# An S5 block and an adaptive-norm attention layer: another way through the last layer norm, and the last four heads in one group

## The chip, the cores and the metric

The kernel runs on one core of a Trainium2 chip. The metric is the device time of one execution in microseconds (us), lower is better. TensorE (PE in the profile, with PEld for its weight loads), VectorE (DVE), ScalarE (ACT) and GpSimd (POOL) each work through their own queue in order; SyncE (SP) issues the DMAs. Results of TensorE land in PSUM[...].

## The reference

The input is x of shape (2, 2048, 512) and a condition vector for each of the two batches. A first layer (a state-space block and a feed-forward with GELU) makes `hidden`. The second layer is what the change touches, and of it only what follows the attention:

```python
att = softmax(q @ k.T) / D ** 0.5            # 16 heads of width 32
out = (att @ v) joined over heads
out = out @ Wp.T + bp
h1  = out + hidden
h2  = gamma * ((h1 - mean) / sqrt(var + EPS) * ln_g + ln_b) + beta
return h2 + h1
```

Mean and variance are those of a row of 512 features; gamma and beta come from the condition vector. Written with one row g = gamma * ln_g and one row t = gamma * ln_b + beta for each batch, the output is (h1 - mean) * rstd * g + h1 + t.

## The kernel before

**Phases.** The first layer runs up to about 1480 us. Then attention runs over 64 blocks, each one batch, one pair of heads and one chunk of 512 queries: 32 blocks of the first batch, 32 of the last. At the end of the last batch the blocks are reordered, so that its chunks 0, 1 and 2 are complete before chunk 3.

**Slots.** A block takes 8 slots (`NP`). Slot j = 8 n + i is slot i of block n. In a slot, in program order: what is due at j, `make` (PE scores `s`, VectorE subtracts the maximum out of PSUM into `pT`; not in slots 0 and 4), `across` (PE `m`, VectorE reduces it, L785), `exponentials` on ScalarE, `keep` for the block 15 slots ahead (PE scores, ScalarE copies them to SBUF, L766, VectorE takes the running maximum, L771; twice in slots 0 and 4, and with no maximum in slot 1), another `exponentials`, what is due at j + 0.5 (`closing`), `take_off` on GpSimd (L814, the kept scores of the next slot), and `weighted` (PE `o`, L835, for the slot before). Every engine's queue is in this order. `after(j, f)` puts a step at the head of slot j, `closing(j, f)` near its end.

**Maxima.** `turn_run` turns the running maximum by four PE transposes per head into a PSUM bank and VectorE reduces it (L792), for head 0 of block n at slot 8n - 6 (slot 2), for head 1 at 8n - 4 (slot 4). `spread` at 8n - 3 (slot 5) turns the negated maximum again (L802) and sends it through DRAM to all partitions as `shift`, which `take_off` needs.

**PSUM.** The tag "pt" is one bank with one buffer. `turn_run`, `spread`, the projection `py` of the first batch and `z` share it: each waits until the one before has been read. "m" is one buffer too, for `across` and for the last batch's `py`; "s" has two.

**Last norm of a tile (128 rows).** `fetch` loads the outputs of all heads (`o4`), the inverted sums (`by`, four DMAs) and `hidden` (`xr`). `divide` multiplies on GpSimd. `project` makes four products with `wp`. `residual` adds on VectorE into SBUF. `statistics` takes mean and variance and the start of an inverse square root. `newton` makes one turn in three 128x1 ScalarE activations, in all nine and one for the shift; `last_norm` writes z = (h - mean) * rstd on ScalarE into a "pt" bank; `gain` multiplies z by g and adds h on VectorE; `close` adds t on GpSimd and issues the output DMA.

**Where they are due.** The 16 tiles of the first batch are closed during the last batch's blocks: two tiles in three blocks, 24 blocks in all. The last batch's own tiles 0 to 11 follow each other every two slots in its last blocks (k, k + 2, ...): the products of one at slot k + 3, ScalarE's Newton at the ends of k + 3 and k + 4, z at the end of k + 4, the gain at k + 5 or its end, close at the end of k + 6.

**The end.** The last chunk's four tiles are projected apart (`end_*`): heads 12 and 13 are divided by GpSimd and projected as a group of their own (`end_project(i, [NG - 1])`), heads 14 and 15 come straight from the last block's PSUM output, are inverted on VectorE (L1037) and multiplied with a weight tile that has zeros elsewhere (L1047). Then come statistics, `rsqrt` on VectorE, z on ScalarE in place, gain and addition.

Of the kernel before, what the change touches and what calls it, by code (L numbers as in the profile page):

```python
# [39 lines left out]
def tile_s5_block_then_sln_attention(  # L40
# [48 lines left out]
    four = const.tile([P, NB], F32, name="four")  # L89
    one_half = const.tile([P, 1], F32, name="one_half")  # L90
    nc.gpsimd.memset(one_half, 1.5)

# [783 lines left out]
    def fetch(b, qt):  # L876

        at = slice(qt * P, (qt + 1) * P)
        o4 = work.tile([P, NG, P], F32, name="o4")
        nc.sync.dma_start(o4, od[b][:, at].rearrange("(g r) q -> r g q", r=P))  # L880
        by = work.tile([P, NG, P], F32, name="by")
        heads = invd[b][:, at].rearrange("(g j) q -> j g q", j=4)
        for j in range(4):
            nc.sync.dma_start(
                by[32 * j : 32 * j + 32, :, :], heads[j : j + 1, :, :].to_broadcast([32, NG, P])
            )
        xr = work.tile([P, D], F32, name="xr", bufs=4)
        nc.sync.dma_start(xr, x2[b][at, :])
        held[b, qt] = o4, by, xr
# [19 lines left out]
    def residual(b, qt):  # L909

        o4, h, py = held[b, qt]
        nc.vector.tensor_add(h, py, h)
        held[b, qt] = h

    def statistics(b, qt):

        h = held[b, qt]
        st = small.tile([P, 6], F32, name="st3")
        nc.vector.bn_stats(st, h)
        mv = small.tile([P, 2], F32, name="mv3")  # L920
        nc.vector.bn_aggr(mv, st)
        v = small.tile([P, 1], F32, name="v3")
        y = small.tile([P, 1], F32, name="scale3", bufs=4)
        shift = small.tile([P, 1], F32, name="shift3", bufs=4)
        nc.vector.tensor_scalar(v, mv[:, 1:2], EPS, None, ALU.add)
        nc.vector.tensor_scalar(
            y.bitcast(I32), v.bitcast(I32), -0.5, float(0x5F3759DF), ALU.mult, ALU.add
        )
        nc.vector.tensor_scalar(v, v, -0.5, None, ALU.mult)
        nc.vector.tensor_scalar(shift, mv[:, 0:1], -1.0, None, ALU.mult)  # L930
        held[b, qt] = h, y, shift, v

    def newton(b, qt, turns, final):

        h, y, shift, v = held[b, qt]
        for _ in range(turns):
            c = small.tile([P, 1], F32, name="c3")
            nc.scalar.activation(c, y, AF.Identity, scale=y)
            nc.scalar.activation(c, c, AF.Identity, bias=one_half, scale=v)
            nc.scalar.activation(y, c, AF.Identity, scale=y)  # L940
        if final:
            nc.scalar.activation(shift, shift, AF.Identity, scale=y)

    def last_norm(b, qt):

        h, scale, shift, _ = held[b, qt]
        z = ps.tile([P, CH], F32, name="z", tag="pt")
        nc.scalar.activation(z, h, AF.Identity, bias=shift, scale=scale)
        held[b, qt] = h, z

    def gain(b, qt):

        h, z = held[b, qt]
        nc.vector.tensor_tensor(z, z, ending[b][0], ALU.mult)
        nc.vector.tensor_tensor(h, z, h, ALU.add)

    def close(b, qt):

        h, z = held.pop((b, qt))
        nc.gpsimd.tensor_tensor(h, h, ending[b][1], ALU.add)  # L960
        nc.sync.dma_start(out[b, qt * P : (qt + 1) * P, :], h)

# [8 lines left out]
    def end_fetch():  # L971
# [9 lines left out]
        for t in range(TT):  # L981
            at = slice((LC * TT + t) * P, (LC * TT + t + 1) * P)
            nc.sync.dma_start(ends["h"][t // 2][:, t % 2, :], x2[LB][at, :])
        late = P - 2 * HD
        nc.gpsimd.memset(ends["o"][1][late:, 1, :], 0.0)
        nc.gpsimd.memset(ends["w"], 0.0)
        nc.gpsimd.tensor_copy(ends["turn"], ident)
        for e in range(2):
            to, of = 3 * HD * e, HD + HD * e
            nc.sync.dma_start(ends["w"][to : to + HD, :], wp[late + HD * e : late + HD * e + HD, NG - 1, :])  # L990
            nc.gpsimd.tensor_copy(ends["turn"][:, to : to + HD], ident[:, of : of + HD])

    def end_fetch_more():
        cols = slice(LC * CH, (LC + 1) * CH)
        nc.sync.dma_start(ends["o"][1][: P // 2, 1, :], od[LB][D - P : D - P // 2, cols])

    def end_divisors(heads):
        cols = slice(LC * CH, (LC + 1) * CH)
        for j in heads:
            at = slice(HD * (j % 4), HD * (j % 4) + HD)  # L1000
            nc.sync.dma_start(
                ends["by"][j // 8][at, j // 4 % 2, :], invd[LB][j : j + 1, cols].to_broadcast([HD, CH])
            )

    def end_divide(g, rows=P):
        o, by = ends["o"][g // 2][:rows, g % 2, :], ends["by"][g // 2][:rows, g % 2, :]
        nc.gpsimd.tensor_tensor(o, o, by, ALU.mult)
# [19 lines left out]
    def end_last(o):  # L1027
        raw, inv, on = (spare(n)[:, 0, :] for n in ("raw4", "inv4", "on4"))
        turned = ps.tile([P, 2, 2 * P], F32, name="turned", tag="pt")
# [6 lines left out]
        for i, at in enumerate(parts):  # L1036
            nc.vector.reciprocal(inv[:, at], turned[:, i, :])  # L1037
            nc.vector.tensor_tensor(on[:, at], o[:, at], inv[:, at], ALU.mult)
        end_project(1, list(range(NG - 1)))
        for i in range(2):  # L1040
            end_project(i, [NG - 1])
        mv = small.tile([P, TT, 2], F32, name="mv4")
        hts = [spare("ht01"), spare("ht23")]
        g_row, t_row = ending[LB]
        for i in range(2):
# [4 lines left out]
            for t in (2 * i, 2 * i + 1):  # L1050
                st = small.tile([P, 6], F32, name="st3")
                nc.vector.bn_stats(st, ends["py", i][:, t % 2, :])
                nc.vector.bn_aggr(mv[:, t, :], st)
            nc.scalar.copy(hts[i], ends["py", i])
        v = small.tile([P, TT], F32, name="v4")
        scale = small.tile([P, TT], F32, name="scale4")
        shift = small.tile([P, TT], F32, name="shift4")
        nc.vector.tensor_scalar(v, mv[:, :, 1], EPS, None, ALU.add)
        rsqrt(v, scale, TT)
        nc.vector.scalar_tensor_tensor(shift, mv[:, :, 0], -1.0, scale, ALU.mult, ALU.mult)  # L1060
        for t in range(TT):
            z = ends["py", t // 2][:, t % 2, :]
            nc.scalar.activation(
                z, z, AF.Identity, bias=shift[:, t : t + 1], scale=scale[:, t : t + 1]
            )
        for t in range(TT):
            qt = LC * TT + t
            y, z = hts[t // 2][:, t % 2, :], ends["py", t // 2][:, t % 2, :]
            nc.vector.tensor_tensor(z, z, g_row, ALU.mult)
            nc.vector.tensor_tensor(y, z, y, ALU.add)  # L1070
            (nc.gpsimd if t < TT - 1 else nc.vector).tensor_tensor(y, y, t_row, ALU.add)
            nc.sync.dma_start(out[LB, qt * P : (qt + 1) * P, :], y)

# [34 lines left out]
    FIRST = -AHEAD - 8  # L1108
    SPREAD = -3
    OPEN = -4  # L1110
# [4 lines left out]
    for n in range(N):  # L1115
        after(max(FIRST + 1 + n, NP * n - AHEAD - 6), load_q, n)
        after(NP * n - AHEAD + NP + 1, turn_run, n, 0)
        after(NP * n - AHEAD + NP + 3, turn_run, n, 1)
        after(NP * n + SPREAD, spread, n)
    for b in range(NB):  # L1120
        for c in range(NQ):
            j = NP * (blocks.index((b, NPAIR - 1, c)) + 1) + 1
            if (b, c) == (LB, LC):
# [7 lines left out]
                after(j + 4, invert, b, c, rest, 32)  # L1131
                after(j + 5, end_divisors, range(NH - 4, NH - 2))
                for g in range(NG - 1):
                    after(j + 3 + g, end_divide, g)
                after(j + 8, end_divide, NG - 1, P // 2)
                after(j + 6, end_begin, 0)
# [7 lines left out]
            for t in range(TT):  # L1144
                qt = c * TT + t
                if b == LB:
# [5 lines left out]
                    after(k + 3, statistics, b, qt)  # L1152
                    closing(k + 3, newton, b, qt, 2, False)
                    closing(k + 4, newton, b, qt, 1, True)
                    closing(k + 4, last_norm, b, qt)

                    (after if (k + 5 - SPREAD) % NP == 0 else closing)(k + 5, gain, b, qt)
                    closing(k + 6, close, b, qt)
                else:

                    k = NP * (NPAIR * NQ * (b + 1) + 2 + 3 * qt // 2) + 3
                    after(k - 2, fetch, b, qt)
                    after(k + 2, divide, b, qt)
                    for g in range(NG):
                        after(k + 3 + g, project, b, qt, (g,))
                    closing(k + 6, residual, b, qt)
                    closing(k + 7, statistics, b, qt)
                    for i in range(3):
                        closing(k + 8 + i, newton, b, qt, 1, i == 2)

                    k += 2 if t % 2 else 8
                    closing(k + 10, last_norm, b, qt)
                    closing(k + 11, gain, b, qt)
                    after(k + 13, close, b, qt)

# [119 lines left out]
```

## Time and profile before

| what | us |
| --- | --- |
| median of three runs | 3533.81 (3532.12 to 3534.32) |
| the profiled execution, its own time | 3533.44 |
| its span, from the first to the last instruction | 3531.7 |
| PE, VectorE, ScalarE, GpSimd busy in the span | 3378.7, 2204.6, 1976.7, 1943.5 |
| PE's share of the chain that ended last | 71% |

The span is what the trace covers; the profiled execution's own time is 1.7 us longer. A busy share is an average over very different stages. In the attention PE and VectorE are both nearly full; what one stage costs is read from stretches of it. A line of the timeline gives start, duration, engine, line of the kernel, operation, output and inputs, shape and, in brackets, how long the engine idled before it and what ended that. A line of the waits gives who waited for whom, us in total, how often, and the longest.

### The profile page before, as it was taken

How to read it: one execution, taken by the hardware profiler on the slowest of the kernel's cores; microseconds unless marked ns; L12 is line 12 of the kernel's file. 1: busy time of each engine (PE TensorE's matmuls, PEld its weight loads, DVE VectorE, ACT ScalarE, POOL GpSimd, SP SyncE). 2: the span in 40 equal slices, each digit the busy share in tenths (PEclk: the TensorE clock that was granted, in tenths of full speed). 3: DMA queues.
4: the chain of work that ended last, by engine and by line, in shares of the span. 5: the costliest groups of instructions: out<-in, count | busy, mean ns of one | idle time of the engine just before them, and what ended most of it. 6: DMA issues, size and time to landing. Idle time of an engine off the chain costs nothing.

```text
span 3531.7 us, 34142 instructions
## 1 busy us (share of the span) xinstructions
PE 3378.7 (96%) x11772; PEld 1534.2 (43%) x11772; DVE 2204.6 (62%) x2937; ACT 1976.7 (56%) x2430; POOL 1943.5 (55%) x982
## 2 busy tenths in 40 slices
PE   7999999999999999899999999999999999999977
PEld 4444444444444444444444444444444444444432
DVE  6233232323232212689999999998888888888864
ACT  2111111111111111488888888888888888888865
POOL 4223131313131311288877888888687787777764
PEclk8999999999999999999999999999999999999999
DMA  8001111111111012332213222222233333323222
GB/s 298 1 30 42 48 39 45 39 50 37 48 36 42 33 45 74 99 71 65 71 50 73 71 65 65 53 72 66 68 85 84 81 76 79 88 71 80 61 89 93
DMA packets 201542, 236.92 MB, mean 67 GB/s; under 512 B 89755, under 2 KB 118939, under 8 KB 197273
## 3 DMA queue, kind: packets, MB, share of 16 engines
q1 hardware_dynamic: 201368, 234.74, 23.9%
q8 instruction: 93, 1.52, 0.2%
q14 instruction: 81, 0.66, 0.1%
HBM read 166.77 MB, written 67.76 MB: 66 GB/s over the span
## 4 chain that ended last, share of the span: by engine, by line
PE 71%; DVE 14%; ACT 11%; issue 2%; DMA 1%; POOL 1%; SPq 0%; DVEq 0%; ACTq 0%; POOLq 0%
PE o L835 14%; PE ph L489 13%; PE po L502 12%; PE s L755 9%; DVE run L771 8%; PE pk L532 6%; ACT x L766 4%; PE pv L544 3%; PE py L906 3%; ACT x L825 3%; PE m L780 2%; ACT pT L825 2%; DVE pT L820 2%; PE pt_run L791 2%; PE pu L423 2%
## 5 line engine op out<-in xcount | busy, mean ns | idle before, releaser
L814 POOL TENSOR_TENSOR x<-x,shift 128x1024 f32<-128x1024 f32 x640 | 1502.7, 2388 | 343.4 <-DMA shift<-flat 269.4
L766 ACT COPY x<-s 128x1024 f32<-128x1024 f32 x640 | 633.7, 1011 | 234.0 <-PE s L755 232.3
L755 PE MATMUL s<-qs,ks 128*128 128x512 f32 x2048 | 703.1, 433 | 51.7 <-DVE run L771 46.8
L825 ACT ACTIVATE x<-x 128x1024 f32<-128x1024 f32 x640 | 675.9, 1057 | 6.7 <-POOL x L814 6.6
L771 DVE TENSOR_TENSOR run<-s,run 128x1024 f32<-128x1024 f32 x512 | 625.4, 1221 | 82.1 <-ACT x L766 64.4
L835 PE MATMUL o<-x,v 128*64 128x512 f32 x2560 | 664.2, 614 | 2.0 <-ACT raw L844 2.0
L820 DVE TENSOR_TENSOR pT<-s,shift 128x1024 f32<-128x1024 f32 x384 | 467.6, 1218 | 55.0 <-PE s L755 50.4
L785 DVE TENSOR_REDUCE top<-m 128x1 f32<-128x768 f32 x512 | 485.8, 949 | 25.7 <-PE m L780 25.4
L755 PEld LDWEIGHTS s<-qs,ks 128*128 128x128 f32 x2048 | 344.9, 189 | 312.2 <-DVE run L771 143.3
L489 PE MATMUL ph<-fT,w_sb 128*128 128x512 f32 x1024 | 462.5, 596 | 0.0
L502 PE MATMUL po<-w_sb,hid 128*128 128x512 f32 x1024 | 460.3, 592 | 0.0
L825 ACT ACTIVATE pT<-pT 128x1024 f32<-128x1024 f32 x384 | 407.0, 1060 | 50.2 <-DVE pT L820 50.2
L493 ACT ACTIVATE hid<-ph,vec 128x512 f32<-128x512 f32 x128 | 87.9, 687 | 595.1 <-PE ph L489 595.1
L835 PE MATMUL o<-pT,v 128*64 128x512 f32 x1536 | 395.2, 593 | 3.8 <-ACT pT L825 3.8
L160 DVE SCALAR_TENSOR_TENSOR lo<-pk,vec,hi 128x512 fp32r<-128x512 f32 x64 | 48.1, 751 | 503.3 <-ACT hi L159 497.4
L780 PE MATMUL m<-ks,qs 128*128 128x384 f32 x1024 | 285.8, 360 | 16.3 <-DVE top L785 14.4
L489 PEld LDWEIGHTS ph<-fT,w_sb 128*128 128x128 f32 x1024 | 193.0, 192 | 228.2 <-issue 228.2
L502 PEld LDWEIGHTS po<-w_sb,hid 128*128 128x128 f32 x1024 | 190.7, 190 | 221.5 <-issue 221.5
L159 ACT ACTIVATE hi<-pk,vec 128x512 fp32r<-128x512 f32 x64 | 44.0, 687 | 393.3 <-PE pk L532 388.8
L436 POOL TENSOR_TENSOR m<-m,m 128x512 f32<-128x512 f32 x8 | 13.1, 1643 | 448.9 <-DVE m L434 448.9
L835 PEld LDWEIGHTS o<-x,v 128*64 128x64 f32 x2560 | 138.5, 135 | 260.7 <-issue 146.3
L512 POOL TENSOR_TENSOR x<-x,gated 128x512 f32<-128x512 f32 x32 | 39.6, 1268 | 354.3 <-DVE gated L511 354.3
(252 smaller groups left out, 2857.9 us busy)
## 6 DMA issues: line engine op xcount, KB each, us to landing
ks<-kd SPq DMA_DIRECT2D x128, 256.0 KB
qs<-qd SPq DMA_DIRECT2D x512, 64.0 KB
shift<-flat SPq DMA_DIRECT2D x64, 512.0 KB
x<-in_x SPq DMA_DIRECT2D x8, 1024.0 KB
w_sb<-in_w SPq DMA_DIRECT2D x8, 1024.0 KB
x<-x SPq DMA_DIRECT2D x8, 1024.0 KB
kd<-hi SPq DMA_DIRECT2D x32, 256.0 KB
kd<-lo SPq DMA_DIRECT2D x32, 256.0 KB
```

What stands on the lines that cost most here:

```text
L489: nc.tensor.matmul(ph, w1_sb[:, k, f * P : (f + 1) * P], fts[b, c][:, k, :], start=k == 0, stop=k == KC - 1)
L502: nc.tensor.matmul(pos[b, c][:, t, :], hid[:, t * P : (t + 1) * P], w2_sb[:, f, :], start=f == 0, stop=f == FC - 1,)
L532: nc.tensor.matmul(pk, w[:, k, g * P : (g + 1) * P], hT[:, k, :], start=k == 0, stop=k == KC - 1)
L755: nc.tensor.matmul(s[:, e, :], kst[pair_of[n], e][:, kt * P : (kt + 1) * P], qst[n][:, e, :], start=True, stop=True,)
L766: nc.scalar.copy(x, s)
L771: nc.vector.tensor_tensor(runs[n], s, kept[n, 0] if kt == 1 else runs[n], ALU.max)
L780: nc.tensor.matmul(m[:, i, :YW], qst[n][:, e, t * P : (t + 1) * P], kst[pair_of[n], e][:, k : k + YW], start=True, stop=True,)
L785: nc.vector.tensor_reduce(tops[n][:, j, 0:1], m[:, :, :YW], AX.XY, ALU.max, negate=True)
L814: nc.gpsimd.tensor_tensor(x, x, shifts[n], ALU.add)
L820: nc.vector.tensor_tensor(x, s, shifts[n], ALU.add)
L825: nc.scalar.activation(x, x, AF.Exp)
L835: nc.tensor.matmul(outs[n][64 * e : 64 * e + 64, :], v[:, kt, e : e + 2, :], x[:, e, :], start=first, stop=final,)
```

## The change

For the first batch, h stays in the PSUM tile of its projection. VectorE makes w = (h - mean) * g (into the buffer of `o4`) and ht = h + t (into that of `xr`); GpSimd makes the three Newton turns in six 128x1 operations; ScalarE scales w by rstd once; GpSimd adds w and ht. z and its bank are gone. The tile's steps are moved: first product in slot 5 (at its end), the second and third at the ends of slots 6 and 7, the fourth at the head of slot 0, residual and statistics at the end of slot 0, `gain` at the end of slot 1, GpSimd's turns in slot 3, `scaled` at the end of slot 4, `close` in slot 6.

For the last batch's tiles 0 to 11, Newton is on VectorE (`deviation`, seven 128x1 operations at slot k + 4), z on ScalarE and the multiply by g on VectorE are issued together at k + 5, into a new SBUF tile y, and GpSimd makes both additions at k + 6.

In all blocks the first `turn_run` is one slot later (slot 3). At the end, the last four heads form one group of 128 rows: the divided heads 12 and 13 stand in the middle 64 rows, the inverted heads 14 and 15 in the outer ones, so that the separate group's products go. The last norm has the same form as the first batch's, with Newton on GpSimd in 13 128x4 operations.

```diff
@@ tiles
-        xr = work.tile([P, D], F32, name="xr", bufs=4)
+        xr = work.tile([P, D], F32, name="xr", bufs=3)
@@ residual
-        nc.vector.tensor_add(h, py, h)
+        if b == LB:
+            nc.vector.tensor_add(xr, py, xr)
+            held[b, qt] = xr, xr, None
+        else:
+            nc.vector.tensor_add(py, py, xr)
+            held[b, qt] = py, xr, o4.rearrange("p g q -> p (g q)")
@@ newton and what follows
-            nc.scalar.activation(c, y, AF.Identity, scale=y)
-            nc.scalar.activation(c, c, AF.Identity, bias=one_half, scale=v)
-            nc.scalar.activation(y, c, AF.Identity, scale=y)
+    def newton(eng, y, v):
+        for _ in range(3):
+            c = small.tile([P, 1], F32, name="c3")
+            eng.tensor_scalar(c, y, y, v, ALU.mult, ALU.mult)
+            eng.tensor_scalar(y, c, 1.5, y, ALU.add, ALU.mult)
+    def turns(b, qt):
+        newton(nc.gpsimd, *held[b, qt][-2:])
+    def gain(b, qt):
+        h, ht, w, mv, y, v = held[b, qt]
+        nc.vector.scalar_tensor_tensor(w, h, mv[:, 0:1], ending[b][0], ALU.subtract, ALU.mult)
+        nc.vector.tensor_tensor(ht, h, ending[b][1], ALU.add)
+    def scaled(b, qt):
+        nc.scalar.activation(w, w, AF.Identity, scale=y)
+    def close(b, qt):
+        nc.gpsimd.tensor_tensor(ht, w, ht, ALU.add)
+        nc.sync.dma_start(out[b, qt * P : (qt + 1) * P, :], ht)
+    def deviation(b, qt):
+        newton(nc.vector, y, v)
+        nc.vector.tensor_scalar(shift, mv[:, 0:1], -1.0, y, ALU.mult, ALU.mult)
@@ last_norm, gain of the last batch
+        nc.scalar.activation(z, h, AF.Identity, bias=shift, scale=scale)
-        nc.vector.tensor_tensor(z, z, ending[b][0], ALU.mult)
-        nc.vector.tensor_tensor(h, z, h, ALU.add)
+        nc.vector.tensor_tensor(y, z, ending[b][0], ALU.mult)
+    def last_close(b, qt):
+        nc.gpsimd.tensor_tensor(h, h, ending[b][1], ALU.add)
+        nc.gpsimd.tensor_tensor(y, y, h, ALU.add)
+        nc.sync.dma_start(out[b, qt * P : (qt + 1) * P, :], y)
@@ end_last
-            nc.vector.tensor_tensor(on[:, at], o[:, at], inv[:, at], ALU.mult)
+            for r in (slice(0, HD), slice(3 * HD, P)):
+                nc.vector.tensor_tensor(on[r, at], o[r, at], inv[r, at], ALU.mult)
         end_project(1, list(range(NG - 1)))
-        for i in range(2):
-            end_project(i, [NG - 1])
...
-        rsqrt(v, scale, TT)
+        nc.gpsimd.tensor_scalar(v, v, -0.5, None, ALU.mult)
+        for _ in range(3):
+            nc.gpsimd.tensor_tensor(c, scale, scale, ALU.mult)
+            nc.gpsimd.tensor_tensor(c, c, v, ALU.mult)
+            nc.gpsimd.tensor_scalar(c, c, 1.5, None, ALU.add)
+            nc.gpsimd.tensor_tensor(scale, scale, c, ALU.mult)
...
+            nc.vector.scalar_tensor_tensor(w, h, mv[:, t, 0:1], g_row, ALU.subtract, ALU.mult)
+            nc.vector.tensor_tensor(ht, h, t_row, ALU.add)
...
+            nc.vector.scalar_tensor_tensor(ht, w, scale[:, t : t + 1], ht, ALU.mult, ALU.add)
@@ due times
-        after(NP * n - AHEAD + NP + 1, turn_run, n, 0)
+        after(NP * n - AHEAD + NP + 2, turn_run, n, 0)
...
-                    closing(k + 3, newton, b, qt, 2, False)
-                    closing(k + 4, newton, b, qt, 1, True)
-                    closing(k + 4, last_norm, b, qt)
-                    (after if (k + 5 - SPREAD) % NP == 0 else closing)(k + 5, gain, b, qt)
-                    closing(k + 6, close, b, qt)
+                    after(k + 4, deviation, b, qt)
+                    after(k + 5, last_norm, b, qt)
+                    after(k + 6, last_close, b, qt)
...
-                    k = NP * (NPAIR * NQ * (b + 1) + 2 + 3 * qt // 2) + 3
-                    after(k - 2, fetch, b, qt)
-                    after(k + 2, divide, b, qt)
-                    for g in range(NG):
-                        after(k + 3 + g, project, b, qt, (g,))
-                    closing(k + 6, residual, b, qt)
-                    closing(k + 7, statistics, b, qt)
-                    for i in range(3):
-                        closing(k + 8 + i, newton, b, qt, 1, i == 2)
-                    k += 2 if t % 2 else 8
-                    closing(k + 10, last_norm, b, qt)
-                    closing(k + 11, gain, b, qt)
-                    after(k + 13, close, b, qt)
+                    k = NP * (NPAIR * NQ * (b + 1) + 2 + 3 * qt // 2)
+                    after(k, fetch, b, qt)
+                    after(k + 3, divide, b, qt)
+                    for g in range(3):
+                        closing(k + 5 + g, project, b, qt, (g,))
+                    after(k + 8, project, b, qt, (3,))
+                    closing(k + 8, residual, b, qt)
+                    closing(k + 8, statistics, b, qt)
+                    closing(k + 9, gain, b, qt)
+                    after(k + 11, turns, b, qt)
+                    closing(k + 12, scaled, b, qt)
+                    after(k + 14, close, b, qt)
```

## The prediction

> **What bounds the kernel now.** I read the busy time by stretch first, one block of 8 slots per stretch, cut at the raw copies of L844. Columns: stretch, its length, busy us (instructions) of PE, PEld, DVE, ACT, POOL, then clock, DMA share, GB/s.
>
> ```profile
> 2152.37:2181.10 28.73, 28.20 (x123) 12.80 (x122) 26.16 (x27) 25.65 (x29) 23.51 (x11) 1.00 0.16 42
> 2570.50:2601.90 31.40, 30.91 (x129) 13.89 (x128) 27.47 (x29) 25.89 (x30) 29.07 (x14) 1.00 0.25 72
> 2601.90:2635.10 33.20, 32.16 (x132) 14.33 (x130) 28.21 (x34) 28.49 (x40) 22.64 (x11) 1.00 0.35 76
> 2635.10:2668.60 33.50, 30.21 (x125) 13.05 (x124) 29.18 (x36) 29.84 (x42) 24.84 (x12) 1.00 0.15 44
> ...
> 3354.70:3412.20 57.50, 46.35 (x153) 19.56 (x153) 39.95 (x64) 41.25 (x74) 31.70 (x17) 0.94 0.28 86
> 3412.20:3461.90 49.70, 36.60 (x117) 13.32 (x117) 23.31 (x49) 31.54 (x63) 34.99 (x24) 0.93 0.42 124
> ```
>
> A block that closes nothing takes 28.73 us with PE busy 28.20 and VectorE 26.16: both are nearly full. In the second batch three blocks carry two tiles of the first batch's last norm and take 31.40 + 33.20 + 33.50 = 98.1, where three plain ones take 86.3: 11.8 us more, 8 times over. The last two lines are the last batch's closing stage: far over PE's busy time.
>
> Next, VectorE's timeline shows which instruction makes a block longer: L785 runs once per slot, so the distance between two of its starts is the slot. First a plain block, then the third of the three, same slots.
>
> ```profile
> 2154.24 0.95 DVE L785 TENSOR_REDUCE top<-m 128x1 f32<-128x768 f32 x1
> 2156.48 0.69 DVE L792 TENSOR_REDUCE top<-pt_run 128x4 f32<-128x512 f32 x1 [1.29 <-PE pt_run L791]
> ...
> 2158.22 0.95 DVE L785 TENSOR_REDUCE top<-m 128x1 f32<-128x768 f32 x1
> ...
> 2161.44 0.95 DVE L785 TENSOR_REDUCE top<-m 128x1 f32<-128x768 f32 x1
> ```
>
> ```profile
> 2641.30 0.95 DVE L785 TENSOR_REDUCE top<-m 128x1 f32<-128x768 f32 x1
> ...
> 2643.30 0.68 DVE L919 BATCH_NORM_STATS2 st<-xr 128x6 f32<-128x512 f32 x1
> ...
> 2645.87 0.95 DVE L785 TENSOR_REDUCE top<-m 128x1 f32<-128x768 f32 x1
> ...
> 2656.98 0.95 DVE L785 TENSOR_REDUCE top<-m 128x1 f32<-128x768 f32 x1
> ...
> 2660.63 0.69 DVE L954 TENSOR_TENSOR z<-z,g_row 128x512 f32<-128x512 f32 x1
> ```
>
> Slot 1 has the only hole of a plain block, 1.29 us. Statistics in slot 2 stretch 3.22 to 4.57, by 1.35 of their 1.44 us: no cover. The residual in slot 1 (2637.27 to 2641.30, 4.03 against 3.98) costs 0.05 of 0.68: it sits in the hole. ScalarE's Newton turns, two slots on (2645.87 to 2653.52, 7.65 against 7.60), cost 0.05 of 2 us: the cover there is ScalarE's spare 3 us a block. z and the gain after it (2656.98 to 2663.09) cost 6.11 against 3.34, 2.77. A product of the projection (2620.37 to 2624.68) costs 4.31 against 3.45, 0.86; the fourth of a tile, in slot 1, 0.35. So two tiles make 2 x (3 x 0.86 + 0.35) + 2 x 1.4 + 2.77 + 0.25 (the odd tile's gain, in the hole) = 11.7, all of the 11.8. VectorE's place in the block is what costs, not ScalarE's load.
>
> For the last batch I asked who PE waits for (3354 to 3462), and for the end the chain of waits.
>
> ```profile
> PE pt_run L791 <- DVE xr L955: 10.2, 4, 3.5
> PE pt_neg L802 <- DVE xr L955: 7.7, 2, 4.7
> ```
>
> ```profile
> 3504.34 8.58 PE py L1022 x20
> 3512.93 1.73 PE py L1047 x4
> ...
> 3518.35 0.18 DVE scale L120
> 3520.58 0.76 ACT py L1063
> ...
> 3527.86 0.69 DVE ht L1071
> ```
>
> 17.9 us are PE waiting for the gain, because z sits in the one "pt" bank that the transposes need.
>
> [...] VectorE's maximum waits for ScalarE's copy of the same scores (0.55 us, once a block). [...] the residual and gain in PSUM should cost no more; the trace has 690 ns (L954, PSUM) and 692 (L955). [...]
>
> **First batch, part by part.** Per tile ScalarE loses nine turns' operations, the shift and z (0.28 + 0.39 + 0.29 three times, 0.29, 0.77: 4.0 us) and gets one 128x512 activation, taken as z's 0.77. Since Newton cost 0.05 this earns about nothing by itself; what goes is the gain's wait for z. VectorE keeps its amount, residual 0.68 + statistics 1.3 + gain 1.4 = 3.4, but all of it now stands at the ends of slots 0 and 1. The hole of 1.3 takes its share, 2.1 are left. Following the queues: slot 1's make comes 2.0 late, slot 2's score waits for its buffer and its m for the reduction, but the transposes (0.65 on PE) have left slot 2, and by slot 5 the delay is 1.75 per tile. Bounds: 1.2 if the small gaps later in the block (0.55, 0.20, 0.12) are used too; 2.45 if none is and the scaling on ScalarE, next to exponentials that PE waits for (0.36), shows. The four products stand in slots 5, 6, 7 and 0: 4 x 0.86 = 3.44 instead of 2.93. Sum for two tiles 2 x (1.75 + 3.44) = 10.4 against 11.7: 1.3 less, times 8 = **10.5 us less** (bounds 21 less to 0).
>
> GpSimd gets six 1-column operations, at 0.21 to 0.4 each 1.3 to 2.4 us a tile; with the division earlier in the same slot it falls up to 2.8 us back at the sixth subtraction of a block, whose result waits some 5 us for its exponential: hidden. SP: six fetches move ahead of the raw copies' DMAs, waiting for nothing; the output DMA waits for close in slot 6, after the shift's DMAs of slot 5.
>
> **The first transposes, one slot later in nearly all blocks.** VectorE's 0.69 leaves the hole for slot 3. But without them PE makes slot 2's scores 0.65 earlier, VectorE starts that slot 0.57 earlier, and at slot 3 both stand where they stood: 0, bounds 0 to 0.65 a block.
>
> **Last batch, 12 tiles.** The multiply now follows z at once at the head of a slot, while PE does the next tile's four products; VectorE idles 2 to 5 us there anyway. The bank is free before any transpose: 17.9 us go. New is Newton on VectorE in front of a slot's make: seven dependent 1-column operations at 0.19 from start to start, 1.33 us. The make, the reduction and the maximum queue behind it, and PE's next products need the m bank after that reduction, about 0.85 us late by the queues at full load; some tiles have no maxima any more: 12 x 0.5 = 6. The gain's second 0.69 leaves VectorE for GpSimd, which gets 12 x 1.27; in 3412 to 3462 it then has about 39 us of work, so that stretch can't fall below that. Net **12 less** (bounds 18 less, none). With three xr buffers a fetch waits for the close three tiles back, in the same slot; that close is ready a slot earlier, so 0, at worst within these bounds.
>
> **The end.** Eight of the 20 products of L1022 go: 8 x 0.43 = 3.4; the VectorE path that they would uncover ends at 3508.8, plus 0.8 for two more partial multiplies, about when the twelve left end (3509.5). From the seed at 3518.5 VectorE now does 8 x 0.71 + 4 x 0.71 = 8.5 against 10.0 to the end: 1.5. GpSimd's 13 small operations (2.7 to 5.2 us) lie beside the first eight (5.7). The last division becomes two of 32 rows (1.26 each, as for 64 rows), behind the last close: done about 3505, wanted at 3509. end_fetch drops two memsets (0.52 each) for two more small DMAs on SP, nine slots before their use: 0. **4.9 less** (4 to 5.5).
>
> **Sum.** 10.5 + 12 + 4.9 = 27.4. The profiled execution took 3533.4 for a span of 3531.7; its median neighbours 3533.8. 3533.4 - 27.4 = **3506**.
>
> **Rivals.** (a) The first batch gives nothing (VectorE's 2.45, products uncovered) and the last about half: 3533.4 - 6 - 4.9 = 3522. For it: VectorE is full in the slots after slot 1. Against: 2.77 of z and gain are surely gone. 0.20. (b) More is hidden in both, the products' fourth too: 3490. 0.15. (c) ScalarE was the limit after all: 16 tiles x 3.2 on top, 3455. Its 29.84 busy in 33.50 speaks for it, the 0.05 against. 0.05. (d) The slower side: the hole in slot 1 stays empty when the transposes leave it, because slot 2's scores can't start earlier; then VectorE's reduction costs up to 0.65 in each of some 60 blocks, 39 us: 3545. It decides from 0.46 a block. The saturated slots speak for it, the 0.65 that PE gains in slot 2 against. 0.08. (e) The new path isn't shorter at the end because GpSimd's small operations take over 0.44 each: 2 to 3 us only, inside the range.
>
> **Numbers.** The forecast, 3496 to 3516, has 0.52. With most of (a) and (b) the range is 3487 to 3525. A change of 0.2% (7 us) is about what can be told from none: faster 0.86, same 0.07, slower 0.07.
>
> **What would show it.** Right: plain blocks stay at 28.8; three blocks sum to about 96.7, the second above 33 and the third near 31.5; no PE wait on the multiply for pt_run in the last batch; L1022 in the end's chain x12. Wrong: plain blocks at 29.2 or more (d); a triple at 98 (a) or below 94 (b, c); in the last batch PE waiting for GpSimd's divisions.

## The result and the profile after

The changed kernel takes 3501.49 us (median of four runs, 3499.28 to 3502.91) against 3532.97 (3532.08 to 3534.32) for the kernel before: a ratio of 0.991, 95% interval 0.9893 to 0.9927. Its profiled execution took 3499.28 for a span of 3497.5, 34.2 us less than the span before. The busy time by stretch, cut at the raw copies (now L842), with the columns as before; first a plain block, then the second and third of three blocks that close two tiles of the first batch, then the last batch's closing blocks:

```profile
2149.50:2178.30 28.80, 28.27 (x123) 12.90 (x121) 26.16 (x27) 25.75 (x29) 23.54 (x11) 1.00 0.14 42
...
2599.90:2633.70 33.80, 32.37 (x130) 14.22 (x131) 29.05 (x35) 26.64 (x30) 26.93 (x19) 1.00 0.24 59
2633.70:2664.00 30.30, 28.84 (x122) 12.65 (x122) 29.00 (x35) 26.48 (x30) 22.86 (x16) 1.00 0.35 75
...
3338.50:3388.10 49.60, 44.19 (x154) 18.21 (x153) 42.60 (x84) 29.35 (x33) 38.46 (x22) 1.00 0.34 100
3388.10:3427.10 39.00, 35.05 (x119) 12.74 (x120) 28.38 (x69) 19.38 (x23) 35.66 (x24) 1.00 0.49 132
3427.10:3473.10 46.00, 38.69 (x116) 13.92 (x114) 20.83 (x50) 17.47 (x20) 35.33 (x23) 0.93 0.37 108
```

The plain block hasn't moved (28.8). With the first of the three, 32.2, the blocks that close two tiles sum to 96.3 where they took 98.1. The last batch's long stretches are 49.6 and 39.0 where they were 57.5 and 49.7, but the one after them grew from 39.7 to 46.0. Most of that growth is work that now falls behind the cut: the stretch holds 22 matmuls of the tiles' projections instead of 16, the first of the four holds 9 instead of 16, and PE is busy for 38.69 instead of 33.82 in the last. PE's idle time in the last grew from 5.9 to 7.3. Summed between the raw copies that bound each stage, from the two traces:

| stage | before | after | difference | predicted |
| --- | --- | --- | --- | --- |
| 24 blocks that close the first batch | 784.4 | 771.9 | -12.5 | -10.5 |
| last four stretches before the end | 187.2 | 172.1 | -15.1 | -12 |
| from the last raw copy to the end | 30.1 | 24.4 | -5.7 | -4.9 |
| everything else | 2530.0 | 2529.1 | -0.9 | 0 |

In the kept traces the first layer and the first block of attention differ by up to 5 us, though no edit touches them; the experiments are therefore read by these stage sums, and their times only beside them.

VectorE's timeline of the third of the three blocks, with the residual, the reductions of slots 1 and 2 (L783, one per slot) and the first half of the new gain:

```profile
2634.71 0.69 DVE L914 TENSOR_TENSOR py<-py,xr 128x512 f32<-128x512 f32 x1
...
2637.98 0.95 DVE L783 TENSOR_REDUCE top<-m 128x1 f32<-128x768 f32 x1
2638.84 0.74 DVE L946 SCALAR_TENSOR_TENSOR o<-py,mv,g_row 128x512 f32<-128x512 f32 x1
...
2641.23 0.95 DVE L783 TENSOR_REDUCE top<-m 128x1 f32<-128x768 f32 x1
```

Residual and statistics lengthen the slot that ends at 2637.98 from 5.11 to 7.25, by 2.14; the gain fills the hole (2637.98 to 2641.23 is 3.25, where a plain block now takes 3.44); up to slot 5 the delay shrinks further, and the block ends 1.61 over a plain one. In the last batch PE waited before for the division in the last of the four stretches, besides the gain (columns: waiting and waited for, us in total, times, longest):

```profile
PE py L906 <- POOL o L893: 2.8, 1, 2.8
```

and now it waits for these:

```profile
PE o L833 <- ACT pT L823: 5.9, 6, 1.4
PE py L904 <- POOL o L891: 5.4, 1, 5.4
```

The 17.9 us of waits for the gain are gone. The single wait for a division on GpSimd has grown from 2.8 to 5.4, in the stretch that grew. The chain at the end:

```profile
3475.84 5.15 PE py L1043 x12
...
3486.42 0.17 DVE scale L1077
```

Twelve products stand where 20 stood, and the seed comes 13.3 us after the last raw copy instead of 16.7.

### The profile page after: what moved, and what is told of

It reads as the page before. It is cut to its first block, busy times and chain, and to the rows that moved or that the text cites. A ratio compares the mean times of both kernels' runs of the same rounds, so it can differ in the third digit from the quotient of the medians.

```text
span 3497.5 us, 34111 instructions
## 1 busy us (share of the span) xinstructions
PE 3369.2 (96%) x11764; PEld 1531.6 (44%) x11764; DVE 2207.6 (63%) x2976; ACT 1894.2 (54%) x2144; POOL 1988.5 (57%) x1098
## 4 chain that ended last, share of the span: by engine, by line
PE 71%; DVE 18%; ACT 7%; issue 2%; DMA 1%; POOL 1%; SPq 1%; DVEq 0%; ACTq 0%; POOLq 0%
PE o L833 14%; PE ph L487 13%; PE po L500 13%; DVE run L769 10%; PE s L753 9%; PE pk L530 6%; ACT x L764 3%; PE pv L542 3%; PE py L904 3%; PE m L778 3%; DVE pT L818 2%; DVE top L783 2%; PE pu L421 2%; PE pt_run L789 1%; ACT pT L823 1%
## 5 line engine op out<-in xcount | busy, mean ns | idle before, releaser
L812 POOL TENSOR_TENSOR x<-x,shift 128x1024 f32<-128x1024 f32 x640 | 1504.3, 2393 | 267.5 <-DMA shift<-flat 227.6
L753 PE MATMUL s<-qs,ks 128*128 128x512 f32 x2048 | 681.0, 423 | 39.8 <-DVE run L769 35.1
L823 ACT ACTIVATE x<-x 128x1024 f32<-128x1024 f32 x640 | 676.2, 1057 | 12.5 <-POOL x L812 12.5
L783 DVE TENSOR_REDUCE top<-m 128x1 f32<-128x768 f32 x512 | 485.7, 949 | 39.6 <-PE m L778 39.1
```

Source lines behind the costliest of these rows:

```text
L753: nc.tensor.matmul(s[:, e, :], kst[pair_of[n], e][:, kt * P : (kt + 1) * P], qst[n][:, e, :], start=True, stop=True,)
L783: nc.vector.tensor_reduce(tops[n][:, j, 0:1], m[:, :, :YW], AX.XY, ALU.max, negate=True)
L812: nc.gpsimd.tensor_tensor(x, x, shifts[n], ALU.add)
L823: nc.scalar.activation(x, x, AF.Exp)
```

## The experiments

### Which part of the first batch's rewriting pays

The prediction said that ScalarE's Newton cost about nothing where it was, and that the gain's wait for z was what went. Four kernels make a square of the two parts, and a fifth moves the turns. T1, T2 and T3 stand for the theories of an expectation. One part is Newton's engine; the other, called the places, is all the rest of the first batch's rewriting: h kept in PSUM, no z, the new slots of the steps and of the transposes. In `first_on_act`, after's places are kept and Newton is ScalarE's again:

```diff
-        newton(nc.gpsimd, *held[b, qt][-2:])
+        act_newton(*held[b, qt][-2:], 1)
...
-                    after(k + 11, turns, b, qt)
+                    for i in range(3):
+                        closing(k + 9 + i, turns, b, qt)
```

> The changed kernel, but the first batch's Newton turns stand on ScalarE again (nine activations a tile, one turn at the end of each of slots 1, 2 and 3). Theory 1 (what counted was where VectorE's work stands and that nothing waits for z): ScalarE's turns are hidden as before, 0 to 3 us above the changed kernel, three blocks with two tiles stay at 96.3 to 96.7. Theory 2 (ScalarE's load was the limit and its relief is the gain): 16 tiles x 3.2 us come back in good part, at least 10 us more, three blocks above 97.6.

It took 3512.48 us (ratio to before 0.9944, 0.9927 to 0.996), and the 24 blocks 784.4: to the tenth what they took before. So T1 is out: the new places, with Newton on ScalarE, give nothing. ScalarE's timeline in the second of three blocks shows why:

```profile
2608.73 1.06 ACT L825 ACTIVATE pT<-pT 128x1024 f32<-128x1024 f32 x1 [1.41 <-DVE pT L820]
2609.69 0.28 ACT L946 ACTIVATE c<-scale 128x1 f32<-128x1 f32 x1
...
2610.62 1.04 ACT L825 ACTIVATE x<-x 128x1024 f32<-128x1024 f32 x1
```

VectorE's residual and statistics, which stand in front of the make, leave ScalarE idle for 1.41, and for the next 15 us no line of it has an idle time in front: ScalarE now follows without slack, and each turn (0.93, from 2609.69 to 2610.62) is in the way. The second and third blocks take 34.6 and 31.2 where the changed kernel has 33.8 and 30.3.

`first_act_later` puts the same turns where the kernel before had them:

```diff
-                        closing(k + 9 + i, turns, b, qt)
-                    closing(k + 12, scaled, b, qt)
-                    after(k + 14, close, b, qt)
+                        closing(k + 11 + i, turns, b, qt)
+                    closing(k + 14, scaled, b, qt)
+                    after(k + 16, close, b, qt)
```

> As first_on_act, with ScalarE's three Newton turns two slots later (slots 3, 4 and 5, where the kernel before had them), the scaling and the close two slots later as well. T1 (place: the turns cost only because in slots 1 to 3 they stand in front of exponentials that are already late by VectorE's 3.4 us): the three blocks go from 98.0 back to 96.4 to 96.8, and the time to 3500 to 3503. T2 (amount: once the hole of slot 1 is filled, ScalarE follows VectorE without slack to the end of the block, so a microsecond more per turn counts wherever it stands): 97.7 to 98.5, time 3510 to 3516. The prediction's 0.05 per pair of turns belongs to T1.

It took 3516.22 us (0.9954, 0.9939 to 0.9969), and the blocks 784.9. That is T2: the amount counts, not which of these slots it stands in.

The fourth corner is `pool_newton_alone`, the kernel before with Newton on GpSimd and nothing else:

```diff
-                    for i in range(3):
-                        closing(k + 8 + i, newton, b, qt, 1, i == 2)
+                    after(k + 9, turns, b, qt)
...
+    def turns(b, qt):
+        h, y, shift, v = held[b, qt]
+        for _ in range(3):
+            c = small.tile([P, 1], F32, name="c3")
+            nc.gpsimd.tensor_scalar(c, y, y, v, ALU.mult, ALU.mult)
+            nc.gpsimd.tensor_scalar(y, c, 1.5, y, ALU.add, ALU.mult)
+        nc.gpsimd.tensor_scalar(shift, shift, y, None, ALU.mult)
```

> The kernel before with one thing changed: the first batch's three Newton turns and the shift's scaling on GpSimd, in slot 4, instead of ScalarE in slots 3 to 5; z stays on ScalarE, the gain on VectorE where it was. The fourth corner of a square: 24 blocks with closing work took 784.4 before, 771.9 after, 784.4 with the new places but Newton on ScalarE. T1 (the prediction's reading: in the old places ScalarE's Newton costs 0.05 a pair, the gain's wait for z costs): 783 to 785, time 3529 to 3534. T2 (ScalarE's load is what the change relieves, whatever the places): 771 to 775, time near 3521. T3 (each is worth about half): 777 to 780.

It took 3514.85 us (0.9953, 0.9937 to 0.997), and the blocks 767.2. That is T2, and more than the 771 to 775 it asked for:

| 24 blocks, us | Newton on ScalarE | Newton on GpSimd |
| --- | --- | --- |
| places of before | 784.4 | 767.2 |
| places of after | 784.4 (later: 784.9) | 771.9 |

Taking Newton off ScalarE gives 17.2 in the old places and 12.5 in the new; once it is off, the new places cost 4.7. The mechanism stands in the kernel before, on a line that the prediction's excerpt left out. VectorE there, third block, in front of the gain:

```profile
2659.49 1.22 DVE L771 TENSOR_TENSOR run<-s,run 128x1024 f32<-128x1024 f32 x1 [1.56 <-ACT x L766]
```

and ScalarE at that moment:

```profile
2656.25 0.28 ACT L938 ACTIVATE c<-scale 128x1 f32<-128x1 f32 x1
...
2657.31 0.29 ACT L942 ACTIVATE shift<-shift,scale 128x1 f32<-128x1 f32 x1
...
2658.46 0.99 ACT L766 COPY x<-s 128x1024 f32<-128x1024 f32 x1
```

The 1.56 us in front of the running maximum wait for ScalarE's copy of a score, which stands behind four small operations (2656.25 to 2657.51), an exponential and, further up, two more turns; ScalarE hasn't idled since 2646.05. In `pool_newton_alone` the same line of VectorE has no bracket:

```profile
2653.43 1.23 DVE L771 TENSOR_TENSOR run<-s,run 128x1024 f32<-128x1024 f32 x1
```

The third block goes from 33.5 to 31.7. The slot that holds this wait and the gain took 6.11 from reduction to reduction and now takes 4.55; in a plain block it is 3.34. So the 2.77 that the prediction booked to z and gain were 1.2 of gain and 1.56 of a backlog of ScalarE that came due there. Why the new places cost 4.7, 0.6 in three blocks, was not taken apart further.

### The transposes one slot later

`turn_back` is the changed kernel with the first transposes in slot 2 again:

```diff
-        after(NP * n - AHEAD + NP + 2, turn_run, n, 0)
+        after(NP * n - AHEAD + NP + 1, turn_run, n, 0)
```

> The changed kernel, but the first transposes stand in slot 2 again. Theory 1 (the hole that they filled in slot 1 is now taken by the norm's VectorE work, which then meets their reduction): about 0.5 us more for each of 16 tiles, and plain blocks back from 28.75 to 28.79: 7 to 10 us more. Theory 2 (their place is indifferent, PE and VectorE shift together): within 2 us of the changed kernel.

It took 3537.58 us (1.0012, 1.0006 to 1.0019): 36 more than the changed kernel, and slower than before. Both expectations are far off. The 31 plain blocks of the first batch take 28.78 in the mean, 28.79 in the changed kernel, so there the move is worth 0; the 24 closing blocks take 813.3 instead of 771.9. PE's timeline in the second of three blocks:

```profile
2610.10 1.04 PE L789 MATMUL pt_run<-ident,run 128*128 128x128 f32 x4 [2.79 <-DVE xr L947]
```

With h kept in PSUM until the gain at the end of slot 1, a transpose at the head of slot 2 finds the "pt" bank taken: 2.79 us of PE, once per tile, twice in three blocks. The stretch around this wait in the busy time by stretch, and the same stretch around the first tile's wait, which is as long (2.80, up to 2509.63):

```profile
2608.80:2613.80 5.00, 3.70 (x12) 2.76 (x14) 3.71 (x5) 1.39 (x3) 4.90 (x5) 0.66 0.18 52
```

```profile
2508.33:2513.33 5.00, 3.70 (x18) 1.90 (x18) 4.25 (x6) 2.84 (x4) 4.90 (x5) 1.00 0.19 52
```

The granted clock is 0.66 in the one and 1.00 in the other. Of the 16 tiles' waits 14 (2.8 us, one 3.1) came with a lower clock and two, of 2.8 as well, did not; what decides between them is not shown. Over the executions time and mean clock go together: six of the 20, with a mean granted clock of 0.987 to 0.989, took 3528.98 to 3532.93 us, the other fourteen, with 0.984 to 0.986, took 3537.21 to 3543.2. The two waits without a lower clock tell the parts of the cost. With wait and lower clock the second and third blocks take 36.6 and 33.2 us, where the changed kernel has 33.8 and 30.3. With the wait alone a second block takes 35.1 and a third 31.7 (the changed kernel has 31.2 at this one place and at most 30.7 at the others), and PE is busy for 31.9 in that second block instead of 33.3. So the wait costs about 1.3 us a tile and the lower clock 1.5 more; over 16 and 14 tiles this makes about 21 and 21, an estimate from these lengths, of the 41 us. The move is no saving of its own but what the new places need.

### The last batch: where Newton belongs, and what gave the gain back

`last_on_act` leaves z and the multiply together at k + 5 and gives Newton back to ScalarE:

```diff
-                    after(k + 4, deviation, b, qt)
+                    closing(k + 3, deviation, b, qt, 2, False)
+                    closing(k + 4, deviation, b, qt, 1, True)
```

> The changed kernel, but the last batch's Newton stands on ScalarE again (two turns at the end of slot k + 3, one and the shift at the end of k + 4), z and the multiply stay together at k + 5. Theory 1 (the gain of this stage is the free pt bank; Newton on VectorE costs about 0.5 us a tile): 2 to 6 us less than the changed kernel. Theory 2 (taking Newton off ScalarE is what the stage gained): 10 us or more above it.

It took 3508.45 us (0.9933, 0.9919 to 0.9948); the four stretches take 178.6 instead of 172.1, 6.5 more. T1, which wanted it faster, falls, and T2 promised 10 or more. PE waits:

```profile
PE o L835 <- ACT pT L825: 12.9, 7, 3.1
```

The turns stand in front of exponentials that PE waits for (12.9 against 5.9), while the wait for the division is gone. All PE waits of the four stretches sum to 21.9 against 19.5; the other 4 us are PE's busy time, 156.6 against 152.3, at clocks of 0.97, 0.90 and 0.95 in the last three stretches where the changed kernel has 1.00, 1.00 and 0.93. On VectorE the turns cost less, not nothing.

What made PE's wait for the division longer? In the changed kernel SP issues, one after the other (the queue's own operations, start and duration):

```profile
3418.44 0.43 SPq L998 DMA_DIRECT2D o<-od  x1
...
3429.65 2.52 SPq L1006 DMA_DIRECT2D w<-wp  x4
...
3432.90 0.40 SPq L878 DMA_DIRECT2D o<-od  x1
```

and GpSimd's division waits:

```profile
3439.78 1.26 POOL L891 TENSOR_TENSOR o<-o,by 128x512 f32<-128x512 f32 x1 [6.83 <-DMA od<-raw]
```

`end_fetch` loads the last chunk's data in 23 transfers at one point, 13.8 us of SP's queue (3418.44 to 3432.2, 0.6 each), and a tile's fetch (o<-od at 3432.90, then five more) stands behind them. The release is put down to od<-raw, issued next on the same queue; what the division needs are the tile's own loads just ahead of it. In the kernel before the same fetch stands behind 21 loads that take 13.0 us (3448.85 to 3461.8), and there GpSimd idles 6.27 before the division. The blocks have become shorter, the run of loads has not. `split_fetch` gives `end_fetch` in five pieces, at slots -1, 1, 2, 3 and 4 of the last block:

```diff
-                after(j - 1, end_fetch)
+                for g in range(NG - 1):
+                    after(j - 1 + g + (g > 0), end_fetch, g)
+                after(j + 3, end_fetch_rows)
+                after(j + 4, end_fetch_weights)
```

> The changed kernel, but the last chunk's 23 loads, which stood together in SP's queue one slot before the last block, stand in five pieces (slots -1, 1, 2, 3 and 4 of the last block). Theory 1 (in the last block PE waits for a division whose loads stand in SP's queue behind those 23): PE's wait of 5.4 us for the division goes, 4 to 6 us less than the changed kernel. Theory 2 (GpSimd's added work is late there): no change, within 2 us.

It took 3494.05 us (0.9893, 0.9877 to 0.991), 7 less than the changed kernel; the last stretch is 42.7 instead of 46.0, and the four sum to 168.7 instead of 172.1. So of the 6.8 between the two profiled spans (3490.7 against 3497.5) half is this; the other half is there before these stretches open and isn't the edit's. PE's waits in the last two stretches:

```profile
PE py L904 <- POOL o L891: 1.8, 1, 1.8
```

5.4 has become 1.8. A rival was GpSimd's load itself. `less_pool` is the changed kernel with the addition of h on VectorE, behind the multiply:

```diff
+        nc.vector.tensor_tensor(y, y, h, ALU.add)
...
-        nc.gpsimd.tensor_tensor(h, h, ending[b][1], ALU.add)
-        nc.gpsimd.tensor_tensor(y, y, h, ALU.add)
+        nc.gpsimd.tensor_tensor(y, y, ending[b][1], ALU.add)
```

> The changed kernel, but the last batch's addition of h stands on VectorE again, right behind the multiply, and GpSimd keeps one addition a tile (1.27 us less for each of 12). Theory 1 (loads in SP's queue set the division in the last block): PE's wait of 5.4 us for the division stays, within 2 us of the changed kernel. Theory 2 (GpSimd's added work is late there): the wait goes, 4 to 6 us less.

It took 3501.09 us (0.9911, 0.9899 to 0.9928), and the stretches 172.7: no difference in the sum, though GpSimd is relieved of 12 x 1.27. Inside it there is one: the last stretch falls from 46.0 to 43.8, and the one before it, where VectorE's addition makes exponentials late (a single PE wait of 3.7), grows from 39.0 to 41.9. PE's waits for divisions are 1.4 and 1.8 instead of one of 5.4, as PE itself comes later. GpSimd idles in front of the division as long as ever:

```profile
3440.29 1.26 POOL L891 TENSOR_TENSOR o<-o,by 128x512 f32<-128x512 f32 x1 [7.34 <-DMA od<-raw]
```

So T1's time came, with a smaller wait than it asked for; and it is the loads, not GpSimd's other work, that hold this division. `best` has both edits:

> The changed kernel with both: the loads in five pieces and the addition of h on VectorE. Theory 1: as with the pieces alone, 4 to 7 us less than the changed kernel. Theory 2: as with the addition alone.

It took 3496.64 us (0.9901, 0.9886 to 0.9916), and the stretches 169.1 against 168.7 with the split alone: the relief is worth nothing in the sum there either. PE's last wait for a division goes, and its waits for exponentials grow from 5.9 to 7.9.

`last_no_newton` is `split_fetch` without the three turns, the call of `newton` in `deviation` taken out; the normalization then uses the seed of the inverse root alone:

> split_fetch with the last batch's three Newton turns on VectorE left out (12 tiles are then normed with the seed alone; their six operations each, about 1.7 us, are missing). Sum of the last four stretches between raw copies in split_fetch 168.7. T1 (the prediction's term: 0.5 a tile on the path): 6 less, 162.7, time near 3488. T2 (the turns are wholly on the path, in front of a make whose exponential PE waits for): 1.7 x 12 = 20 less at most, 10 or more. T3 (hidden beside PE's products and the wait for them): within 2 of 168.7.

It took 3489.98 us (0.9883, 0.9867 to 0.99); the four stretches take 161.2, 7.5 less. Its last stretch:

```profile
3425.10:3463.50 38.40, 35.71 (x116) 12.88 (x115) 16.44 (x32) 17.30 (x21) 35.48 (x26) 1.00 0.47 133
```

and that of `split_fetch`:

```profile
3423.60:3466.30 42.70, 38.91 (x117) 14.13 (x116) 20.82 (x50) 17.48 (x21) 36.68 (x26) 0.92 0.45 126
```

PE is 3.2 us less busy there with as many matmuls but one, at a clock of 1.00 instead of 0.92: put down to the clock, an estimate from these two lines (38.91 x 0.92 is 35.8, beside 35.71). What is left for Newton is then 7.5 - 3.2 = 4.3, of which 3.0 in the second of the four (46.6 instead of 49.6), where blocks still need maxima and VectorE was busy 42.6. T1's 6 is the nearest; whether the clock's 3.2 belong to it can't be told.

`late_norm` keeps every operation and moves the last batch's statistics and Newton behind the slot's make:

```diff
-                    after(k + 3, statistics, b, qt)
-                    after(k + 4, deviation, b, qt)
+                    closing(k + 3, statistics, b, qt)
+                    closing(k + 4, deviation, b, qt)
```

> split_fetch with the last batch's statistics and Newton moved from the head of a slot to its second half, behind the make: nothing is taken away, only VectorE's order changes. T1 (PE's waits for exponentials, 3.9 + 1.9 us in the last two stretches, come from statistics and Newton standing in front of the make): the four stretches fall from 168.7 to 162 to 166, time 3488 to 3492. T2 (PE waits because of the residual and the buffers, not because of these): within 1.5 of 168.7. T3 (the norm is then late for the next projection's bank or for the fetch that waits for the close): 171 or more.

It took 3492.6 us (0.9889, 0.9874 to 0.9904), and the stretches 164.5: 4.2 less than `split_fetch` by stage, as T1 said. PE's waits for exponentials have shrunk from 5.9 to 0.5, but those for the residual have grown from 1.6 to 6.0, and those for divisions from 1.8 to 6.0. In sum PE waits only 0.9 less; the rest is its busy time, 149.4 against 152.4 at the same clocks. So the size fits T1, but where the 4.2 arise is not shown.

`late_add` takes one addition a tile from GpSimd there and gives it to VectorE, in the second half of slot k + 5:

```diff
+                    closing(k + 5, add_back, b, qt)
...
-        nc.gpsimd.tensor_tensor(h, h, ending[b][1], ALU.add)
-        nc.gpsimd.tensor_tensor(y, y, h, ALU.add)
+        nc.gpsimd.tensor_tensor(y, y, ending[b][1], ALU.add)
```

> late_norm with the last batch's addition of h on VectorE, in the second half of the slot after the multiply; GpSimd has one 1.27 us addition less per tile. Four stretches in late_norm: 164.5, with 6.0 of PE waits for GpSimd's divisions and GpSimd busy 39.5 of the last 43.3. T1 (GpSimd is now the limit of the last stretch): 3 to 6 less, 158.5 to 161.5, time 3486 to 3490. T2 (the divisions wait for their loads, not for GpSimd): within 1.5 of 164.5. T3 (VectorE's further 0.69 a tile is on the path, as in less_pool's third stretch): 166 or more.

It took 3497.37 us (0.9901, 0.9887 to 0.9916), and the stretches 168.3, 3.7 more. That is T3 by its number (its total, 166 or more); by the waits GpSimd now stands waiting for VectorE's addition with the divisions behind it, and PE's wait for them grows to 7.4. Of the versions with all of Newton, `late_norm` and `split_fetch` are the fastest, both below the changed kernel; 1.5 us between their medians is less than their ranges tell apart. Newton on GpSimd in the old places (767.2) together with `late_norm` was not tried.

### The end alone

`tail_alone` is the kernel before with the new end only (the functions `end_*` and their due times of the diff).

> The kernel before with the end alone changed (the last four heads in one group, last norm with Newton on GpSimd). Theory 1 (eight products of 0.43 us and 1.5 us of the norm): 4.9 us less than before, all of it after the last block's output. Theory 2 (the end is held by transfers, so that the products are hidden): 1.5 us less.

It took 3528.45 us (0.9993, 0.9986 to 1.0), 3.3 below its own before by the medians; the profiled span is 3526.2 against 3531.7. From the last raw copy to the end it takes 24.4 where before took 30.1, as in the changed kernel, so the end's 5.7 stand by themselves; the four stretches ahead of it came out 0.9 longer (188.1). In its chain the twelve products take 5.15 where twenty took 8.58, 3.4 less. The other 2.3 come behind the statistics.

## Why the prediction was right, and for which wrong reason

**The time** is within the forecast's own range, 3496 to 3516, and 4.5 below its 3506.

**Transposes, plain blocks.** Put at 0, measured 0. Rival (d), an empty hole, is out. But their part in the closing blocks stood in half a sentence, without a price: there it is worth 41 us, about half of it with the lower clock by the estimate from `turn_back`.

**First batch.** Put at 10.5, measured 12.5 by the trace. VectorE's delay was followed correctly: 3.4 less the hole leaves 2.1 (2.14 measured), recovered to 1.75 (1.61): 2 x 0.14 x 8 is about the 2 us by which the stage was mis-sized. The four products came at 3.44 (the second block, 5.05 over a plain one, is 1.61 + 3.44). The third block was to be "near 31.5" and is 30.3, because the fourth product of its tile stands ahead of the raw copy that opens it. On the bank VectorE's residual takes 690 ns in the mean (685 before, over both batches) and the gain's two operations 742 and 680 (691 and 692 before). GpSimd's subtraction took 2388 ns before and takes 2393, over all blocks; what VectorE's new operations add to one beside them was not measured. GpSimd's six 128x1 operations were put at 0.21 to 0.4 each: 0.21 is its copy of 128x32 in the kernel before (209 ns), 0.4 was the author's estimate; they take 0.34 and 0.27 in turn, 1.8 a tile. The step that failed is the reading of the kernel before: "VectorE's place in the block is what costs, not ScalarE's load", and from it "this earns about nothing by itself". The turns were priced by the slots in which they stand. Those slots had spare time on ScalarE only in the sense that VectorE hadn't to wait there; the work piled up in ScalarE's queue, was paid up to 12 us later as VectorE's 1.56, and was booked to the gain. Newton's move was the whole gain, 17.2, and the rest of the rewriting took 4.7 back. Rival (c), "ScalarE was the limit after all", had the right engine with a price three times too high: 3.2 a tile, where 17.2 / 16 = 1.1 came. That the sum came out right is no evidence for its terms, and as far as the cause goes it is luck: the sum was made from after's lengths against before's, and both were read well, whatever made before's long.

**Last batch.** Put at 17.9 less 6 for Newton, 12; measured 15.1. The 17.9 went as said. In the sum of PE's waits over these stretches, 32.3 before and 19.5 after, 12.8 less; the other 2.3 are PE's busy time, which in the first long stretch fell from 46.35 to 44.19 for 153 and 154 matmuls, at a clock of 1.00 instead of 0.94. That term was not in the prediction, and no run shows that the change causes it. Newton's 6 was near (4.3, or 7.5 with the clock), though the seven operations occupy VectorE for 1.8 us and not 1.33: with one column operand one takes 0.21 and with two 0.27, and they start 0.25 to 0.31 apart, where 0.19 was taken from operations of 0.15. What was missing is SP's queue. The text counts the fetches it moves, but not that the loads of `end_fetch` (21 in 13.0 us before, 23 in 13.8 now) keep their length when the blocks around them shrink: the wait behind them grew, and spreading them was worth 3.4 us. "PE waiting for GpSimd's divisions" was named as a sign of being wrong, and it came; the cause was the queue, not GpSimd's work (it idles 6.83 in front of that division, and 7.34 in `less_pool`).

**The end.** Put at 4.9, measured 5.7. The products' 3.4 are exact. The other term, 8.5 us from the seed on, was too long because it summed durations: VectorE's twelve operations of 0.68 to 0.74 start 0.59 to 0.67 apart, and take 7.8. GpSimd's turns lie beside the first eight; VectorE's first and last four, and GpSimd's last of thirteen:

```profile
3486.49 0.74 DVE L1092 SCALAR_TENSOR_TENSOR w<-py,mv,g_row 128x512 f32<-128x512 f32 x1
...
3491.52 2.73 DVE L1097 SCALAR_TENSOR_TENSOR ht<-w,scale,ht 128x512 f32<-128x512 f32 x4
```

```profile
3490.11 0.20 POOL L1087 TENSOR_TENSOR scale<-scale,c 128x4 f32<-128x4 f32 x1
```

They end at 3490.31, 1.2 us before they are wanted.

## What to carry to other kernels

A small operation on an engine with some spare time is not free because its own slot keeps its length: follow the queue until it has idled again, and read the bracket of the first wait behind it, on the engine that it feeds (here 1.56 us on VectorE). Price a part of a change by the kernel that has it alone; a sum of before and after can be right with its causes exchanged. When a stage gets shorter, list what in it keeps its length, bursts of DMA issues above all, and spread these (here 23 loads of 13.8 us, worth 3.4).

## What the runs showed of the hardware

- In `turn_back`, of 16 waits of PE of 2.8 to 3.1 us between busy stretches, 14 came with a lower granted clock (0.66 over the 5 us around one of them) and two of 2.8 did not (1.00); four transposes took 1.04 us behind a wait (2610.10, granted clock 0.66) and 0.66 us without one (2618.73, granted clock 1.00), and a second block was 36.6 us long with wait and lower clock and 35.1 with the wait alone.
- At the end of the changed kernel GpSimd's operations on 128x4 take 0.20 to 0.23 us and start 0.27 to 0.31 apart when each needs the one before; thirteen took 3.6 us.
- VectorE's back-to-back 128x512 operations overlap at the end of the changed kernel: the first eight last 4 x (0.74 + 0.68) = 5.68 us in sum, but 5.03 pass from the start of the first to that of the ninth (3486.49 to 3491.52).
- SP's queue took 13.8 us in the changed kernel for the 23 loads of `end_fetch`, 0.6 each, before it issued the tile's fetch behind them; issued in five pieces they cost the stage 3.4 us less.
